# A fused attention and mixture-of-experts kernel: first norms' rows moved to another tile, their transposes to another place in the step, contexts loaded a step sooner, routed products taken from in front of a switch

## The chip, the cores and the metric

The kernel runs on one core of one Trainium2 chip. A core has TensorE (matmuls, called PE in the profile, with its weight loads as PEld), VectorE (DVE), ScalarE (ACT), GpSimd (POOL) and SyncE (SP). SP and POOL also issue DMAs, and each engine works its own instructions in order. The metric is the device time of one execution in microseconds (us); three executions of the kernel before gave 720.6, 720.77 and 722.7, median 720.77.

## The reference

There are 16 batches of 100 tokens with 256 channels, each with a context of 361 rows of 192, and 16 heads of 64.

```python
q = (layernorm(x) @ Wq) heads;  k, v = (ctx @ Wkv) heads
x = x + softmax(q k^T * 64**-0.5) v @ Wproj + bproj
h = layernorm(x)
logits = clip(h @ router_w.T + routing_bias, -50, 50);  probs = sigmoid(logits)
p, sel = top-1 of probs over 7 experts
tw = clip(0.5 + p + 1e-8, 0.5, 2.0)
out = x + 0.5 / tw * swiglu(h, shared) + (p / tw) * swiglu(h, expert sel)
```

`swiglu(h, w1, w2, w3)` is `silu(h @ w1.T) * (h @ w3.T) @ w2.T` with 704 inner channels.

## The kernel before

Everything is fp32. The 1,600 tokens lie in 13 row tiles of 128 (the last has 64), kept in `acc`. `xT` holds the normed tokens transposed, channels on partitions; it feeds the queries, later the router and the shared experts. PSUM is used as eight banks in turn (`bank()`, L125).

**The attention** runs in 32 steps, s = 2b+g: batch b, and g = 0 or 1 for the lower or upper eight heads (L862 to L921). A step has four score products, each for two heads (`scores`, L682). For each, VectorE takes the row maxima (L701), ScalarE the exponentials with their sums (L704), and VectorE then transposes the result in blocks of 32 (L717); that transposing is done one score product later. `moved` (L728) sends the blocks of a whole step through DMAs of SP and POOL into `aT`, which `values` (L750) multiplies with v two steps later for g=0 and one step later for g=1. Between the score products stand products of keys (L611, L632) and values (L611, L659): the keys of batch b+1 and its first value parts in steps with g=1, the rest of the values of b in steps with g=0. So the end of a step with g=0 has three score products in a row. What follows them there, in the order written (PE, ACT, DVE and SP all keep the order in which the code issues):

```python
if g == 0:
    while fillers:            # projections of finished tiles, routers
        fillers.popleft()()
    for _ in range(min(2, len(qs))):
        qs.pop(0)()           # queries, two of four units of two batches
turning(tb)
```

and then `values` of batch b-1, `moved(tb)`, the next context's load (`load_ctx`, L522, at g=1, two batches ahead, into one of two buffers), and `load_later(s)` (L546).

**The norms.** `layer_norm` (L170) returns a list of small parts (moments of each tile, one reciprocal root on POOL, one `normalise` for each tile) and `turn`, the transposes on TensorE (L212) with ScalarE's copies into `xT` (L215). The parts wait in `norms` and are done one after each score product but a step's first, and one at the step's end. When the last part is done, `turn` is put into `turns`; a list of `turns` is worked off at i = 0 of a step with g=0, after the first score product and the product behind it (L899). There are two kinds of norm: the first norm of the input (tiles 0-1, 2-5, 6-8 and 9-12, the last two begun after steps 6 and 9), and the second norm of the attention's result (tiles 0-2, 3-5, 6-8 and 9-12; `keep=True`), whose rows also go to DRAM for the later gather and whose `turn` puts the router (L236) into `fillers`. Both kinds write their rows into `xn`, four buffers in turn (L191). `finished(b)` (L813) puts the projection (L782) of each tile that batch b completes into `fillers`, to be worked off in the next step with g=0.

**The shared experts** follow (`hidden`, `down`, L413 to L508) and overlap with the router of the last group and the sorting of tokens by expert.

**The routed experts** run tile by tile: `run(k)` (L1053) makes the first products of a tile (L1020) into two banks, then the transposes of the next tile's gathered rows (`turn(k+1)`, L976), the rest of the products, and the down product of the tile before (`finish`, L1028). How many tiles there are is data; the kernel reads the number into a register on each engine (L1084) and takes one arm of a `tc.Switch` (L1089), each arm being the whole loop for one number. Before the switch stand, for tile 0, `ahead = turn(0)` between two `down` calls (L1012) and `first_products(0, ahead)` (L1046, L1087): sixteen products.

Of the kernel before, what the change touches and what calls it, by code (L numbers as in the profile page):

```python
# [14 lines left out]
F32 = mybir.dt.float32  # L15
# [7 lines left out]
B, LQ, C = 16, 100, 256  # L23
LKV, CTX = 361, 192
H, DK = 16, 64
I, E = 704, 7
# [38 lines left out]
def xattn_moe(  # L65
# [101 lines left out]

    biases = deque()

    def layer_norm(tiles, keep=False):  # L170


        n = len(tiles)
        of, xns = {}, []

        def moments(i):
            if i == 0:
                of["mv"] = small.tile([P, 4, 2], F32, name="mv")
                of["rstd"] = small.tile([P, 4], F32, name="rstd")
            st = small.tile([P, 6], F32, name="st")  # L180
            nc.vector.bn_stats(st, acc[:, tiles[i], :])
            nc.vector.bn_aggr(of["mv"][:, i, :], st)

        def roots():
            rstd = of["rstd"]
            nc.vector.tensor_scalar(rstd[:, :n], of["mv"][:, :n, 1], EPS, None, ALU.add)
            nc.gpsimd.tensor_tensor(rstd[:, :n], rstd[:, :n], power[:, :n], ALU.pow)

        def normalise(i):
            t = tiles[i]  # L190
            xn = small.tile([P, C], F32, name="xn", bufs=4)  # L191
            nc.vector.tensor_scalar(
                xn,
                acc[:, t, :],
                of["mv"][:, i, 0:1],
                of["rstd"][:, i : i + 1],
                ALU.subtract,
                ALU.mult,
            )
            if keep:  # L200
                nc.sync.dma_start(xn_d[t * P : t * P + rows(t), :], xn[: rows(t), :])
            else:
                biases.append(t)
            xns.append(xn)

        def turn():
            for i in range(0, n, 2):
                tr = bank()
                m = min(2, n - i)
                for o in range(m):  # L210
                    for k in range(2):
                        nc.tensor.transpose(  # L212
                            tr[:, ds((k * m + o) * P, P)], xns[i + o][:, ts(k, P)], ident
                        )
                nc.scalar.copy(  # L215
                    xT[:, :, ds(tiles[i] * P, m * P)],
                    tr[:, : 2 * m * P].rearrange("p (k n) -> p k n", k=2),
                )

        parts = [lambda i=i: moments(i) for i in range(n)] + [roots]  # L220
        return parts + [lambda i=i: normalise(i) for i in range(n)], turn
# [289 lines left out]
    with ExitStack() as attn:  # L511
# [34 lines left out]
        def load_later(s):  # L546

            if 1 < s < 4:
                m = ts(s - 2, NCH // 2)
                nc.sync.dma_start(  # L550
                    wp_sb[:, m], wproj.rearrange("(m p) c -> p m c", p=P)[:, m]
                )
            if s == 3:
                nc.sync.dma_start(rb_sb, rbias.to_broadcast([P, E]))
                nc.sync.dma_start(rw_sb[:, :, :E], rwT.rearrange("(k p) e -> p k e", p=P))
            if s == 4 or s == 7:
                load_x(GROUPS[s // 3 + 1])
            if s == 6 or s == 9:
                normalised(GROUPS[s // 3])
            if 10 <= s < 14:  # L560
                load_shared(s - 10)
            if s in (2 * B - 3, 2 * B - 2):
                load_shared(s - 2 * B + 7)

# [234 lines left out]
        turns, fillers, norms = deque(), deque(), deque()  # L799

        def normalised(g, keep=False):
            parts, turn = layer_norm(g, keep)
            norms.extend(parts)


            def turned():
                turn()
                if keep:
                    fillers.append(lambda: norms.extend(router(g)))

            norms.append(lambda: turns.append(turned))
# [31 lines left out]
        pairs = key_pairs(0)  # L843
        product(pairs)
        product(pairs)
        parts, turn_first = layer_norm(FIRST)
        for one in parts:
            one()
        product(pairs)
# [12 lines left out]
        for s, (b, g) in enumerate(steps):  # L862

            if g == 0:
                pairs = values_of.pop(b)
                if s == 0:
                    ask = lambda: qs.pop(0)() or (lambda: None)
                    pairs[1:] = [ask, ask] + pairs[1:]  # L870
                elif (b + 1) % QG == 0 and b + 1 < B:
                    qs = q_units((b + 1) // QG)
            elif b + 1 < B:
                if b:
                    values_of[b + 1] = value_pairs(b + 1)
                pairs = key_pairs(b + 1)
                for i in (4, 2) if b + 2 < B and b + 1 not in GUESTS else (2,):
                    pairs.insert(i, values_of[b + 1].pop(0))
            else:

                hT0 = ap2.tile([P, NJ, H * DK], F32, name="v")
                hT0 = hT0.rearrange("p j n -> p (j n)")[:, : (NI + 1) * 3 * P]
                hT0 = hT0.rearrange("p (i n) -> p i n", i=NI + 1)
                first = hidden(GROUPS[0], hT0, ap2, 3 * P, SAME)
                pairs = [lambda: first.pop(0)() or (lambda: None) for _ in range(SAME)]
            tb = new_blocks()
            turning = None
            for i in range(n2):
                exponentials, then = scores(b, g * n2 + i)
                if puts:  # L890
                    puts.popleft()()
                exponentials()
                if turning:
                    turning(tb)
                    part()
                turning = then
                for _ in range(-(-len(pairs) // (n2 - i))):
                    product(pairs)
                while g == i == 0 and turns:  # L899
                    turns.popleft()()  # L900
            if puts:
                puts.popleft()()
            if g == 0:
                while fillers:
                    fillers.popleft()()
                for _ in range(min(2, len(qs))):
                    qs.pop(0)()
            turning(tb)
            for _ in range(2 if s < 2 else 1):
                part()  # L910
            if g == 0 and s:
                for at in range(NG):
                    values(b - 1, at, *held.pop(0))
                    after_values()
                finished(b - 1)
            held.append(moved(tb))
            if g == NG - 1 and b + 2 < B:
                cTs[b + 2] = load_ctx(b + 2)
            if g == NG - 1:
                host(b)  # L920
            load_later(s)  # L921
# [62 lines left out]
    with tc.tile_pool(name="hs", bufs=1) as hs:  # L984
        def run_hidden(g):
            n = sum(map(rows, g))
            hT = hs.tile([P, NI + 1, n], F32, name=f"hT{n}")
            for piece in hidden(g, hT, sp):
                piece()
            return hT  # L990

        parts, turn_last = layer_norm(GROUPS[-1], keep=True)
        for one in parts:
            one()
        hT = run_hidden(GROUPS[1])
        turn_last()
        down([(3, hT, 0)])
        for one in router(GROUPS[-1]):
            one()
        down([(5, hT, 2), (4, hT, 1)])  # L1000
        fill = sort_tokens(hs)
        for k in range(NW):
            fetch(k)
        hT2 = run_hidden(GROUPS[2])
        fill()
        for k in range(NX - 1):
            gather_into(xgs, xn_d, k)
        hT3 = run_hidden(GROUPS[3])
        down([(6, hT2, 0), (7, hT2, 1)])
        down([(12, hT3, 3)])  # L1010
        down([(9, hT3, 0), (10, hT3, 1)])
        ahead = turn(0)  # L1012
        down([(8, hT2, 2), (11, hT3, 2)])
    hp = ctx.enter_context(tc.tile_pool(name="hp", bufs=2))

# [27 lines left out]
            oob_is_err=False,  # L1043
        )

    def first_products(k, xgT):  # L1046
        pa, pb = bank(), bank()
        w = wexs[k % NW]
        products(pa, xgT, w, [i * P for i in range(NI - 1)])
        products(pb, xgT, w, [I + HALF + i * P for i in range(NI - 1)])  # L1050
        return pa, pb

    def run(k, state, tiles):  # L1053


        xgT, last, made = state
        w, hT = wexs[k % NW], hTs[k % 2]
        pa, pb = made or first_products(k, xgT)
        pc = bank()
        n = (NI - 1) * P  # L1060
        s = sp.tile([P, n], F32, name="sg")
        nc.scalar.activation(s, pa[:, :n], AF.Silu)
        nc.vector.tensor_tensor(
# [15 lines left out]
            gather_into(bgs, base_d, k + NX - 1)  # L1079
        if k and k + NW - 1 < tiles:  # L1080
            fetch(k + NW - 1)
        return ahead, (k, hT, bgs[k % NX]), None

    n = nc.values_load(e_at[:, NS:], min_val=0, max_val=NS - NF)  # L1084
    for k in range(NX - 1):
        gather_into(bgs, base_d, k)
    first = ahead, None, first_products(0, ahead)  # L1087

    for extra in tc.Switch(n, NS - NF + 1):  # L1089
        then = first  # L1090
# [57 lines left out]
```

## Time and profile before

| | us |
|---|---|
| median of three executions | 720.77 |
| the profiled execution | 721.24 |
| its span, first to last instruction | 719.4 |
| ScalarE, exponentials (L704) | 142.0 |
| VectorE, block transposes (L717) | 132.9 |
| VectorE, maxima (L701) | 123.5 |
| TensorE, keys (L611, 361 columns) | 125.8 |
| TensorE, values' products (L611, 512 columns) | 126.2 |
| TensorE, scores (L688) | 99.2 |
| TensorE, routed products (L1020) | 78.3 |
| TensorE, transposes of normed tiles (L212) | 7.4 |

The last projection of the attention ends at 521 us, the shared experts at 596, and the routed tiles fill the rest. The granted TensorE clock averages 0.995 of full speed. In a list by time, a row gives the start, the duration, the engine, the line, the tiles as out<-in, the shapes and how many instructions were merged; in brackets is the time that the engine was idle before and what ended it. TensorE's matmuls are pipelined, and each fp32 product of the program shows as two, so a row's duration overlaps the next: for what a matmul costs the distance from start to start is read.

### The profile page before, as it was taken

The numbers are of one execution on the slowest core, as the hardware profiler recorded it, in microseconds if no ns is written. First come the engines' busy times: TensorE is split into PE (matmuls) and PEld (weight loads), VectorE is DVE, ScalarE is ACT, GpSimd is POOL, SyncE is SP. The second block draws the span as 40 slices with busy tenths as digits, with TensorE's granted clock in tenths as the row PEclk, the third lists the DMA queues.
The fourth block names the chain that finished last, engine by engine and source line by source line (L and its number), as shares of the span: only waits on it lengthen the run. The fifth ranks groups of instructions, "written<-read, shape, count | busy, mean of one in ns | idle before, by whom it ended". The sixth has DMA issues, their size and how long they took to land. (4 is left out here: it accounts for less than half of the span.)

```text
span 719.4 us, 14826 instructions
## 1 busy us (share of the span) xinstructions
PE 707.9 (98%) x5192; PEld 510.3 (71%) x5192; DVE 420.5 (58%) x1100; ACT 280.7 (39%) x793; POOL 197.3 (27%) x417
## 2 busy tenths in 40 slices
PE   9999999999999999999999999999999998999996
PEld 6556667667575766757577576755866578999996
DVE  2777766867687576876778778677247222122121
ACT  2564563534545263453644636453022111111110
POOL 4142422322342222323223322233010104343321
PEclk9999999999999999999999999999999999999999
DMA  7055756454474543537354473555104912998860
GB/s 260 23 140 157 178 128 159 95 140 125 106 204 127 166 109 96 139 88 197 93 136 124 109 181 83 142 129 143 52 26 155 382 34 58 326 348 333 309 249 23
DMA packets 55979, 109.23 MB, mean 152 GB/s; under 512 B 28681, under 2 KB 37964, under 8 KB 53972
## 3 DMA queue, kind: packets, MB, share of 16 engines
q1 hardware_dynamic: 45252, 81.79, 37.1%
q0 software_dynamic: 10352, 25.98, 13.8%
q8 instruction: 44, 0.72, 0.4%
q14 instruction: 43, 0.35, 0.2%
q10 hardware_dynamic: 288, 0.39, 0.2%
HBM read 60.81 MB, written 5.35 MB: 92 GB/s over the span
## 5 line engine op out<-in xcount | busy, mean ns | idle before, releaser
L704 ACT ACTIVATE at<-mm,nm 128x361 f32<-128x361 f32 x256 | 142.0, 561 | 173.4 <-DVE nm L701 173.2
L738 POOL DMA_DIRECT2D aT<-tb x256 | 126.1, 500 | 296.7 <-PE mm L760 104.6
L701 DVE TENSOR_REDUCE nm<-mm 128x1 f32<-128x361 f32 x256 | 123.5, 523 | 60.1 <-PE mm L688 59.3
L717 DVE STREAM_TRANSPOSE tb<-at 128x384 f32<-128x384 f32 x256 | 132.9, 558 | 4.5
L611 PE MATMUL mm<-cT,wk_sb 64*128 64x361 f32 x768 | 125.8, 467 | 0.5 <-DMA cT<-in_ctxT 0.4
L611 PE MATMUL mm<-wv_sb,cT 64*128 64x512 f32 (+1 forms) x552 | 126.2, 589 | 0.0
L611 PEld LDWEIGHTS mm<-cT,wk_sb 64*128 64x128 f32 x768 | 75.7, 188 | 45.7 <-issue 5.0
L688 PE MATMUL mm<-kT,qT 64*128 64x361 f32 x512 | 99.2, 479 | 1.7 <-ACT at L704 1.7
L611 PEld LDWEIGHTS mm<-wv_sb,cT 64*128 64x128 f32 (+1 forms) x552 | 53.7, 185 | 53.1 <-issue 43.1
L1020 PE MATMUL mm<-xgT,wex 128*128 128x128 f32 x660 | 78.3, 275 | 0.0
L1020 PEld LDWEIGHTS mm<-xgT,wex 128*128 128x128 f32 x660 | 76.9, 192 | 1.0 <-issue 0.3
L688 PEld LDWEIGHTS mm<-kT,qT 64*128 64x128 f32 x512 | 48.8, 188 | 35.8 <-issue 8.9
L760 PE MATMUL mm<-aT,v 128*64 128x100 f32 (+1 forms) x1472 | 72.5, 251 | 0.5 <-DMA aT<-tb 0.4
L760 PEld LDWEIGHTS mm<-aT,v 128*64 128x64 f32 (+1 forms) x1472 | 67.2, 135 | 4.9 <-issue 3.0
L424 PE MATMUL mm<-xT,w_sb 128*128 128x384 f32 (+1 forms) x176 | 60.9, 503 | 0.0
L424 PEld LDWEIGHTS mm<-xT,w_sb 128*128 128x128 f32 x176 | 32.9, 190 | 26.1 <-issue 8.5
L704 ACT ACTIVATION_READ_ACCUMULATOR at<-mm,nm 128x1 f32 x256 | 50.7, 198 | 0.0
L587 PE MATMUL mm<-xT,wq_sb 128*128 128x200 f32 x256 | 46.9, 336 | 0.0
L587 PEld LDWEIGHTS mm<-xT,wq_sb 128*128 128x128 f32 x256 | 43.4, 190 | 4.0 <-issue 1.5
L792 PE MATMUL mm<-wp_sb,resT 128*128 128x256 f32 x192 | 44.8, 386 | 0.0
L651 ACT COPY kT<-mm 128x361 f32<-128x361 f32 x64 | 29.4, 461 | 39.2 <-PE mm L611 39.2
L792 PEld LDWEIGHTS mm<-wp_sb,resT 128*128 128x128 f32 x192 | 35.9, 191 | 10.3 <-issue 2.5
(154 smaller groups left out, 558.9 us busy)
## 6 DMA issues: line engine op xcount, KB each, us to landing
wex<-in_wex SPq DMA_DIRECT2D x15, 2176.0 KB
aT<-tb POOLq DMA_DIRECT2D x256, 80.2 KB, 3.3
aT<-tb SPq DMA_DIRECT2D x256, 80.2 KB
over<-row SPq DMA_DIRECT2D x64, 100.0 KB
cT<-in_ctxT SPq DMA_DIRECT2D x10, 576.0 KB
cT<-in_ctxT SPq DMA_DIRECT2D x5, 541.5 KB
xn_d<-xn SPq DMA_DIRECT2D x12, 128.0 KB
base_d<-acc SPq DMA_DIRECT2D x12, 128.0 KB
```

The source lines that it names most:

```text
L424: nc.tensor.matmul(to[:, :n], w13_sb[:, k, ds(at, P)], xT[:, k, ds(g[0] * P, n)], start=(k == 0), stop=(k == 1),)
L587: nc.tensor.matmul(pq[:, o, :], wq_sb[:, u, k, ts(o, P)], xT[:, k, ts(g, QG * LQ)], start=(k == 0), stop=(k == 1),)
L611: nc.tensor.matmul(to[o][:height, :width], *operands(o, k), start=(k == 0), stop=(k == NR - 1),)
L651: nc.scalar.copy(kT[:, c, :], to[0][:, :LKV])
L688: nc.tensor.matmul(sc[o][:, :LKV], qTs[b // QG][r, c, ts(b % QG, QB), :], kTs[b][c // 4][r, c % 4, :], start=True, stop=True,)
L701: nc.vector.tensor_reduce(nm[:, o : o + 1], sc[o][:, :LKV], AX.X, ALU.max, negate=True)
L704: nc.scalar.activation(at[:, o, :LKV], sc[o][:, :LKV], AF.Exp, bias=nm[:, o : o + 1], accum_out=sums[:, o : o + 1],)
L717: nc.vector.transpose(tb[:, :, :, o, i * QR : i * QR + 32].rearrange("p j k n -> p k j n"), at[:, o, :].rearrange("p (k j n) -> p k j n", ...
L738: queue.dma_start(aT[ts(j, 32), i].rearrange("p k o n -> p (k o n)"), tb[ts(i, 32), j].rearrange("p k o n -> p (k o n)"),)
L760: nc.tensor.matmul(av[ts(o, DK), i, :], v[:n, ds((2 * c + o) * DK, DK)], aT[:n, :, j, o, ts(i, QR)], start=(j == 0), stop=(j == NJ - 1),)
L792: nc.tensor.matmul(pp[:r, :C], resT[:, c, QP : QP + r], wp_sb[:, c, :], start=(c == 0), stop=(c == NCH - 1))
L1020: nc.tensor.matmul(to[:, ts(o, P)], w[:, ds(j * 2 * I + u, P)], xgT[:, j, :], start=(j == 0), stop=(j == 1),)
```

## The change

It has four parts, which keep the arithmetic and the results as they were.

1. `layer_norm` takes a place instead of a flag. The four first norms write their rows into `w13_sb`, the tile that will hold the shared experts' first weights, its two halves in turn (`places`); the second norms keep `xn`. The four loads of these weights (`load_shared`) move from steps 10 to 13 to steps 20 to 23.
2. `turns` are worked off at the end of a step with g=0, before `fillers`, instead of after the step's first score product. Batch 1 keeps the old place. In the order of instructions this moves five groups of transposes behind the step's last score product: tiles 6-8 within step 10; 9-12 from step 14 to step 12; and of the second norms 0-2 from step 16 to 14, 3-5 from 22 to 20, 6-8 from 30 to 28. A router moves with each of the last three, behind the projection and in front of the queries.
3. A context is loaded at the end of the step with g=0 instead of g=1, except the first (b=0).
4. `first_products` is gone. `turn(0)` stands directly before the switch, the sixteen products inside each arm.

```diff
-    def layer_norm(tiles, keep=False):
+    def layer_norm(tiles, place=None):
         n = len(tiles)
+        keep = place is None
...
-            xn = small.tile([P, C], F32, name="xn", bufs=4)
+            xn = small.tile([P, C], F32, name="xn", bufs=4) if keep else place[:, ts(i, C)]
...
-            if 10 <= s < 14:
-                load_shared(s - 10)
+            if 20 <= s < 24:
+                load_shared(s - 20)
...
-            parts, turn = layer_norm(g, keep)
+            parts, turn = layer_norm(g, None if keep else places.pop(0))
...
-        parts, turn_first = layer_norm(FIRST)
+        places = [w13_sb[:, i % 2, :] for i in (1, 0, 1, 0)]
+        parts, turn_first = layer_norm(FIRST, places.pop(0))
...
-                while g == i == 0 and turns:
+                if b == 1 and g == i == 0:
                     turns.popleft()()
             if puts:
                 puts.popleft()()
             if g == 0:
+                while turns:
+                    turns.popleft()()
                 while fillers:
                     fillers.popleft()()
...
-            if g == NG - 1 and b + 2 < B:
+            if g == (NG - 1 if b == 0 else 0) and b + 2 < B:
                 cTs[b + 2] = load_ctx(b + 2)
...
-        ahead = turn(0)
         down([(8, hT2, 2), (11, hT3, 2)])
...
-    def first_products(k, xgT):
-        pa, pb = bank(), bank()
-        w = wexs[k % NW]
-        products(pa, xgT, w, [i * P for i in range(NI - 1)])
-        products(pb, xgT, w, [I + HALF + i * P for i in range(NI - 1)])
-        return pa, pb
-
     def run(k, state, tiles):
-        xgT, last, made = state
+        xgT, last = state
         w, hT = wexs[k % NW], hTs[k % 2]
-        pa, pb = made or first_products(k, xgT)
-        pc = bank()
+        pa, pb, pc = bank(), bank(), bank()
         n = (NI - 1) * P
+        products(pa, xgT, w, [i * P for i in range(NI - 1)])
+        products(pb, xgT, w, [I + HALF + i * P for i in range(NI - 1)])
...
-    first = ahead, None, first_products(0, ahead)
+    first = turn(0), None
```

More of the change, by code (lines that the diff above doesn't have):

```diff
@@ L990, in run_hidden @@
             return hT
-        parts, turn_last = layer_norm(GROUPS[-1], keep=True)
+        parts, turn_last = layer_norm(GROUPS[-1])
         for one in parts:
@@ L1044, in finish, with run @@
         )
-    def first_products(k, xgT):
-        pa, pb = bank(), bank()
-        w = wexs[k % NW]
+    def run(k, state, tiles):
+        xgT, last = state
+        w, hT = wexs[k % NW], hTs[k % 2]
+        pa, pb, pc = bank(), bank(), bank()
+        n = (NI - 1) * P
         products(pa, xgT, w, [i * P for i in range(NI - 1)])
         products(pb, xgT, w, [I + HALF + i * P for i in range(NI - 1)])
-        return pa, pb
-    def run(k, state, tiles):
-        xgT, last, made = state
-        w, hT = wexs[k % NW], hTs[k % 2]
-        pa, pb = made or first_products(k, xgT)
-        pc = bank()
-        n = (NI - 1) * P
         s = sp.tile([P, n], F32, name="sg")
@@ L1081, in run @@
             fetch(k + NW - 1)
-        return ahead, (k, hT, bgs[k % NX]), None
+        return ahead, (k, hT, bgs[k % NX])
     n = nc.values_load(e_at[:, NS:], min_val=0, max_val=NS - NF)
```

## The prediction

> **What bounds the kernel.** I read the page first for who is busy, then TensorE's waits, then its order of time around each place that the change touches.
>
> ```profile
> PE 707.9 (98%) x5192; PEld 510.3 (71%) x5192; DVE 420.5 (58%) x1100; ACT 280.7 (39%) x793; POOL 197.3 (27%) x417
> ```
>
> ```profile
> PE mm L979 <- DVE hgT L1063: 2.0, 1, 2.0
> PE mm L688 <- ACT at L704: 1.7, 1, 1.7
> ...
> PE mm L611 <- DMA cT<-in_ctxT: 0.4, 2, 0.2
> ```
>
> TensorE works 98% of the span, and the waits that the second view names for it (in all, times, longest) come to some 5 us. So two things count alone: TensorE's own work, and any new wait of TensorE. The chain of waits follows only the last output DMA (712 to 716 us) and tells nothing of the rest. A step is s = 2b+g. Most steps have slack, but the end of a step with g=0 has not: three scores stand there in a row, and their exponentials lag. Step 20 in order of time (start, us, engine, line; in brackets the idle time before and what ended it):
>
> ```profile
> 323.43 1.99 PE L688 MATMUL mm<-kT,qT 64*128 64x361 f32 x12
> 325.35 3.72 PE L792 MATMUL mm<-wp_sb,resT 128*128 128x256 f32 x16
> 328.91 2.87 PE L587 MATMUL mm<-xT,wq_sb 128*128 128x200 f32 x16
> ```
>
> ```profile
> 329.51 0.56 ACT L704 ACTIVATE at<-mm,nm 128x361 f32<-128x361 f32 x1 [1.13 <-DVE nm L701]
> ...
> 330.06 0.55 ACT L704 ACTIVATE at<-mm,nm 128x361 f32<-128x361 f32 x1
> 330.51 0.20 ACT L704 ACTIVATION_READ_ACCUMULATOR at<-mm,nm 128x1 f32 x1
> ```
>
> The scores end at T = 325.35, where the projection starts, but ScalarE ends the last exponential at 330.71, T+5.4. VectorE sets that pace: each of the three needs two maxima (L701) and the two transposes of the one before (L717), about 2 us. I call this distance the lag; steps without norm parts (6, 16, 24) have 4.7.
>
> **A. The stall at step 14 goes: -3.3 us.**
>
> ```profile
> 224.05 1.09 PE L212 MATMUL mm<-ident,xn 128*128 128x128 f32 x8
> 225.07 0.88 PE L688 MATMUL mm<-kT,qT 64*128 64x361 f32 x4
> 227.69 3.06 PE L688 MATMUL mm<-kT,qT 64*128 64x361 f32 x8 [1.75 <-ACT at L704]
> ```
>
> ```profile
> 224.60 0.41 DVE L192 TENSOR_SCALAR xn<-acc,mv,rstd 128x256 f32<-128x256 f32 x1 [3.27 <-PE mm L212]
> ```
>
> ```profile
> 228.00:231.40 3.40, 3.40 (x10) 1.87 (x9) 3.24 (x10) 3.25 (x11) 2.71 (x6) 0.50 0.80 206
> ```
>
> VectorE waits 3.27 us at L192: the four xn buffers still hold tiles 9 to 12, untransposed, when the second norm of tiles 0 to 2 wants one. The maxima behind it come late and TensorE idles 1.75 us (1.9 against its usual spacing); then it runs 228.0 to 231.4 at clock 0.50 (the last-but-two number). Start to start against the usual, that window costs 1.4 more. With the first norms' rows in w13_sb nobody holds those buffers. The moved load_shared lands at steps 20 to 23, eight steps before its use at 31.
>
> **B. Contexts a step sooner: -0.9 us.** At 87.2 and 209.0 the first keys start 0.38 us late and the next ones 0.08. The load goes to the end of g=0, behind that step's aT transfers on SP and in front of host and load_later's own; its buffer's last reader, the values of b, is done by then. It leaves the place behind the aT that the next step needs. The values' aT waits at steps 4 and 12 (0.1 and 0.26) may shrink, and one may appear at step 22, whose cover by transposes and router goes: nothing in sum.
>
> **C. Transposes beside projection and queries: -1.4 us.** Before, the products from values to scores take 257.42 to 260.90 with six transposes between them and 320.85 to 323.43 without: 0.90, and the scores behind them take 2.03 instead of 1.92. So 1.01 for six transposes whose own spacing is 0.11 each, 0.66; the rest, 0.35, is paid where TensorE goes from 64-row tiles to 128-row tiles and back. Beside a projection they pay only 0.66. Four groups save 0.35 each. The fifth leaves step 30, where nothing is saved: the second half of its values starts at 479.46 when the aT of step 29 lands, so TensorE waits there instead. At step 28 its 0.66 and its router's 0.47 (266.58 to 267.04) are paid in full: **+1.1 us**. With each router some eighteen small VectorE operations of 0.13 to 0.29 us and one exponential (0.22) come a batch sooner; they are as many as before and go between steps' products as before, except that those at step 29 can put its aT back by up to 0.4 us, within the wait of step 30. The moved transposes pass nothing on SP or POOL.
>
> **E. The new wait: +8.1 us.** In the listed order of the changed program ScalarE's copies of the transposes (L215) stand behind all four exponentials of the step, and the readers follow on TensorE almost at once: the router's L245 at steps 14, 20 and 28, the queries at step 10, because tokens 600 to 799 reach into tile 6. TensorE gets there at T + 0.71 (transposes) + 3.46 (16 spacings of 0.216) = T+4.17. The copies take 0.59 (two tiles), the second ends 0.84 after the lag, and 0.05 is the way to TensorE.
> - Step 10: lag 5.7 (5.77 before, two moments in the way): 5.7+0.59+0.05 = 6.34, wait 2.2.
> - Step 14: only one normalise left in the loop, lag 5.0: 5.89, wait 1.7.
> - Steps 20 and 28: lag 5.36: 6.25, wait 2.1 each.
>
> Step 12 transposes too, but its queries read tokens 600 to 799, long there: none. Behind the waiting matmul stand the queries and the values, and VectorE's last transpose of the step behind their evacuation; the aT made of it is read two steps later, so only TensorE pays. Nothing hides these waits. Banks: eight in turn; the last of step 20's needs the second exponential, which is done at T+3.0.
>
> **D. The switch: -1.1 us**, unknown in part.
>
> ```profile
> 595.70 3.84 PE L1020 MATMUL mm<-xgT,wex 128*128 128x128 f32 x32
> 601.52 0.41 PE L979 MATMUL mm<-ident,xg 128*128 128x128 f32 x2 [1.99 <-DVE hgT L1063]
> ```
>
> ```profile
> L1144 PEldq COMPARE_BRANCH  x1: 3584/3584/3584, 597.7 to 597.7; - x1
> ```
>
> The idle 1.99 us is the branch: TensorE's sequencer is in it from 597.66 to 601.25, and VectorE had finished at 600.6. It reaches the branch 17 matmuls ahead of the array. The change removes no matmul: 16 products stand behind the branch instead of before it. Is that worse? In front of it now stand 15 matmuls of the shared path, so the branch runs under those. The register load (591.97 before, 0.27 earlier now, as two transposes have left; 0.74 long) ends at 592.44; branch from 592.9 to 596.5, first product at 596.8. ScalarE has the transposed rows copied at 596.3, so that is not last. 3.68 us of products: 600.5 against 601.52. Other end: if the branch begins only when the array has drained (595.8), the products start at 599.9 and it is 2.1 slower. A branch at 709.7 took 0.31 us with matmuls still queued, so I take the early end. The Trainium skill ("TensorE: Matmul & The Clock Gate", Architectural detail) gives TensorE a queue of 64; with that the branch would be hidden wholly and the copy decides, -1.5. The trace's 17 matmuls with their 17 weight loads decide. ScalarE's branch moves behind its copy, to 599.8; its silu is late but not needed before TensorE's second tile.
>
> **F. What the waits do to the clock: +4.5 us.** The same page (HAM oscillation) gives a rule that speaks for the change: no idle gaps above about 3.4 us. By it the waits of E cost themselves alone, and the sum is A+B+C+D+E, +1.1 = **+2.5 us**. The trace says otherwise: 1.75 us idle in a window of 3.41 brought half clock for the next; 1.51 us in another (600.0 to 603.4) did not. So the limit is near half a window. There are five gaps of 1.7 to 2.2 us (steps 10, 14, 20, 28, and about 2 at step 30), and each costs 1.5 if 1.6 us of it fall in one window. For a gap of 2.1 that is (3.41-2.1+2x0.5)/3.41, two in three; for 1.7, half. Three windows of five: 4.5 us; none gives 0, all five 7.5.
>
> **Sum.** Against the profiled run's 721.24 (span 719.4 and 1.8 around it): -3.3-0.9-1.4-1.1+1.1+8.1+4.5 = +7.0, 728.2. The median of the runs shown is 0.5 below that run: **727.7 us**, slower by 1.0%.
>
> **Rivals.**
> - *The clock holds* (none or one half window): 723.3 to 724.8. For it: the page's rule, and window phases differ from run to run. Against: the row of A. 0.20.
> - *The copies aren't late*, and the change is faster: the price is E and F, so 721.24-3.3-0.9-1.4-1.1+1.1-0.5 = 715.1. It decides where the lag is below 3.5 us. All sixteen g=0 steps but the first and step 30 show 3.4 to 5.8, and 3.39 is the stalled step 14; the waits together must stay below 5.6 for no loss. 0.08.
> - *The branch starts after the drain*: 3.2 more, 730.9. 0.12.
> - The forecast, two to four half windows, 726 to 729.5: 0.60.
>
> A measurement tells about 0.3% from no change. Faster by more: 0.08; within (718.6 to 722.9): 0.12, the clock holding with a somewhat smaller wait; slower: 0.80. The range 722 to 732 leaves out the second rival and the worst of the third with five windows.
>
> **To check.** Right: no 3.27 us wait at L192 and no half clock near 228; no wait of L611 for contexts; new waits of L245 three times and L587 once on the xT copy, near 2 us; transposes of three tiles followed by L792; two to four rows at clock 0.50 in the attention; first routed product about 1 us behind the last shared one. Wrong: copies that end before the projection does, or a routed product 4 us late.

## The result, and the profile after

| | before | after | ratio, 95% interval |
|---|---|---|---|
| median, us | 721.38 (719.42 to 722.75) | 731.89 (730.7 to 734.83) | 1.015 [1.0124, 1.0176] |
| profiled execution, us | 721.24 | 730.7 | |
| its span, us | 719.4 | 729.0 | |

Each side has six executions; the three that stand ahead of the prediction are among those of the kernel before. The change makes the kernel 1.5% slower. The forecast was 1.0% slower, 727.7 us. The median lies at the upper edge of the range of 722 to 732, and three of the six executions lie above it (732.75, 732.75 and 734.83 us). In the attention every line number of the changed kernel is one higher than before (L212 is now L213).

The first part of the page, engines' busy time, and then TensorE's waits (engine, line, what it waited for: us in total, times, longest), of the kernel after:

```profile
PE 709.2 (97%) x5192; PEld 509.2 (70%) x5192; DVE 421.7 (58%) x1100; ACT 280.8 (39%) x793; POOL 197.4 (27%) x417
```

```profile
PE mm L213 <- DVE xn L193: 6.5, 5, 2.0
PE mm L761 <- DMA over<-row: 2.0, 1, 2.0
PE mm L588 <- ACT xT L216: 2.0, 1, 2.0
PE mm L132 <- DVE ones L129: 1.1, 1, 1.1
PE mm L213 <- DVE w_sb L193: 0.7, 1, 0.7
PE mm L1024 <- DVE acc L506: 0.7, 1, 0.7
PE mm L246 <- ACT xT L216: 0.6, 1, 0.6
PE mm L1024 <- issue: 0.4, 1, 0.4
```

The number of instructions on each engine is unchanged; the time went into waits. The old ones are gone: no L689 waits for L705 (the stall at step 14), no L612 for a context. The largest new one is not where the forecast put it. The router (L246) waits 0.6 us for ScalarE's copies in the whole kernel, where 5.9 were forecast. It is the transposes themselves (L213) that wait, 7.2 us in six pieces, for rows that VectorE has not written yet (w_sb is the new place of the first norms' rows).

Step 20 in order of time, of the kernel after: TensorE, then VectorE, then ScalarE (start, us, engine, line; idle time before in brackets):

```profile
323.08 0.44 PE L213 MATMUL mm<-ident,xn 128*128 128x128 f32 x2
324.43 0.44 PE L213 MATMUL mm<-ident,xn 128*128 128x128 f32 x2 [0.91 <-DVE xn L193]
326.85 0.41 PE L213 MATMUL mm<-ident,xn 128*128 128x128 f32 x2 [1.98 <-DVE xn L193]
327.09 3.62 PE L793 MATMUL mm<-wp_sb,resT 128*128 128x256 f32 x16
330.64 0.54 PE L246 MATMUL mm<-xT,rw_sb 128*32 128x96 f32 x16
```

```profile
324.01 0.37 DVE L193 TENSOR_SCALAR xn<-acc,mv,rstd 128x256 f32<-128x256 f32 x1
324.30 0.96 DVE L702 TENSOR_REDUCE nm<-mm 128x1 f32<-128x361 f32 x2
325.18 0.15 DVE L715 RECIPROCAL at<-sums 128x2 f32<-128x2 f32 x1
325.37 1.04 DVE L718 STREAM_TRANSPOSE tb<-at 128x384 f32<-128x384 f32 x2
326.33 0.37 DVE L193 TENSOR_SCALAR xn<-acc,mv,rstd 128x256 f32<-128x256 f32 x1
```

```profile
328.23 0.20 ACT L705 ACTIVATION_READ_ACCUMULATOR at<-mm,nm 128x1 f32 x1
328.33 0.86 ACT L216 COPY xT<-mm 128x512 f32<-128x512 f32 x2
```

TensorE has finished its scores at T = 323.08. The first row tile was written a step before and is transposed at once. The second and third are written by VectorE at 324.01 and 326.33, each behind the maxima and block transposes of one of the three last score products. So TensorE, which has run ahead of VectorE here, follows it tile by tile. The copies end at 329.19, T+6.1, as forecast (T+6.2). But TensorE has lost its time already: it reaches the router only at T+7.56, and waits for nothing there.

At step 14, where two of the three tiles were written earlier, TensorE meets both waits, a short one for a row and then one for the copies:

```profile
227.56 0.66 PE L213 MATMUL mm<-ident,xn 128*128 128x128 f32 x4
228.94 0.44 PE L213 MATMUL mm<-ident,xn 128*128 128x128 f32 x2 [0.73 <-DVE xn L193]
229.22 3.62 PE L793 MATMUL mm<-wp_sb,resT 128*128 128x256 f32 x16
233.43 0.54 PE L246 MATMUL mm<-xT,rw_sb 128*32 128x96 f32 x16 [0.59 <-ACT xT L216]
```

Here T is 227.56, and the router starts at T+5.87, where the forecast had put it (5.89).

Stretches of 3.41 us, the kernel after (TensorE's busy time, its granted clock, DMA share, GB/s):

```profile
core 0: us, PE busy (x), PEclk, DMA share, GB/s
321.96:325.38 3.42, 2.00 (x12) 1.00 0.84 239
...
444.84:448.25 3.41, 1.48 (x10) 1.00 0.83 245
448.25:451.66 3.41, 2.44 (x7) 0.50 0.59 152
451.66:455.08 3.42, 3.42 (x9) 0.50 0.11 33
455.08:458.49 3.41, 3.41 (x32) 1.00 0.00 0
485.80:489.21 3.41, 1.37 (x32) 1.00 0.71 181
489.21:492.62 3.41, 3.41 (x35) 0.50 0.47 117
```

Step 28 has the same waits as step 20, and at their end TensorE runs two windows at half clock; the wait at step 30 brings a third. This is one execution, the fastest of the six. The three slower ones have mean granted clocks of 0.990, 0.990 and 0.987, against 0.992 here, so they probably had more such windows; they have no trace to show it.

**Where the 9.6 us of the two spans are.** The distances from a step's first score to the next one's, subtracted between the two traces, give a ledger. What the moved instructions cost is taken from the prediction (six transposes 0.66 beside a projection and 1.01 between scores, eight 0.88 and 1.23, a router 0.47); the remainder is wait or clock. The "half clock in the attention" includes 0.5 us that fall into step 31.

| us | forecast | traces |
|---|---|---|
| stall at step 14 and its half window | -3.3 | -3.9 |
| contexts | -0.9 | -1.0 |
| transposes and routers moved | -0.3 | 0.0 |
| wait at step 10 | 2.2 | 2.2 |
| wait at step 12 | 0 | 0.6 |
| wait at step 14 | 1.7 | 1.7 |
| waits at steps 20 and 28 | 2.1 each | 3.4 each |
| half clock in the attention | 4.5 | 4.5 |
| shared experts, switch and routed tiles | -1.1 | -0.7 |
| first score earlier | - | -0.6 |
| sum | 7.0 | 9.6 |

For step 20 the working is: its tail, from the last score to the next step's first, is 4.55 us longer; transposes and router that came into it cost 1.13; 3.42 are wait. At step 28 it is 7.48 longer: 1.13, the same 3.42, and 2.93 for two half windows. At step 14 the wait is read from the router's start (T+5.87 instead of T+4.17). The first score's start is chance: in the profiles of the kernels below it lies between 0.6 us earlier and 0.4 later than before.

### The profile page after: what moved, and what is told of

The parts are those of the page before. It is cut to its first block, busy times and chain, and to the rows that moved or that the text cites. A ratio compares the mean times of both kernels' runs of the same rounds, so it can differ in the third digit from the quotient of the medians.

```text
span 729.0 us, 14796 instructions
## 1 busy us (share of the span) xinstructions
PE 709.2 (97%) x5192; PEld 509.2 (70%) x5192; DVE 421.7 (58%) x1100; ACT 280.8 (39%) x793; POOL 197.4 (27%) x417
## 5 line engine op out<-in xcount | busy, mean ns | idle before, releaser
L705 ACT ACTIVATE at<-mm,nm 128x361 f32<-128x361 f32 x256 | 141.9, 560 | 172.5 <-DVE nm L702 172.3
L612 PE MATMUL mm<-wv_sb,cT 64*128 64x512 f32 (+1 forms) x552 | 126.1, 589 | 0.0
L612 PE MATMUL mm<-cT,wk_sb 64*128 64x361 f32 x768 | 124.8, 464 | 0.1
L612 PEld LDWEIGHTS mm<-cT,wk_sb 64*128 64x128 f32 x768 | 74.1, 187 | 45.7 <-issue 3.0
L689 PE MATMUL mm<-kT,qT 64*128 64x361 f32 x512 | 97.0, 474 | 0.0
L612 PEld LDWEIGHTS mm<-wv_sb,cT 64*128 64x128 f32 (+1 forms) x552 | 52.9, 185 | 53.9 <-issue 43.6
L689 PEld LDWEIGHTS mm<-kT,qT 64*128 64x128 f32 x512 | 48.1, 187 | 35.8 <-issue 9.8
L705 ACT ACTIVATION_READ_ACCUMULATOR at<-mm,nm 128x1 f32 x256 | 50.4, 197 | 0.0
L588 PE MATMUL mm<-xT,wq_sb 128*128 128x200 f32 x256 | 47.1, 337 | 2.0 <-ACT xT L216 2.0
L588 PEld LDWEIGHTS mm<-xT,wq_sb 128*128 128x128 f32 x256 | 43.1, 190 | 6.4 <-ACT xT L216 2.4
L793 PE MATMUL mm<-wp_sb,resT 128*128 128x256 f32 x192 | 46.7, 399 | 0.0
L793 PEld LDWEIGHTS mm<-wp_sb,resT 128*128 128x128 f32 x192 | 37.7, 201 | 8.5 <-issue 2.5
```

The source lines that it names most:

```text
L588: nc.tensor.matmul(pq[:, o, :], wq_sb[:, u, k, ts(o, P)], xT[:, k, ts(g, QG * LQ)], start=(k == 0), stop=(k == 1),)
L612: nc.tensor.matmul(to[o][:height, :width], *operands(o, k), start=(k == 0), stop=(k == NR - 1),)
L689: nc.tensor.matmul(sc[o][:, :LKV], qTs[b // QG][r, c, ts(b % QG, QB), :], kTs[b][c // 4][r, c % 4, :], start=True, stop=True,)
L705: nc.scalar.activation(at[:, o, :LKV], sc[o][:, :LKV], AF.Exp, bias=nm[:, o : o + 1], accum_out=sums[:, o : o + 1],)
L793: nc.tensor.matmul(pp[:r, :C], resT[:, c, QP : QP + r], wp_sb[:, c, :], start=(c == 0), stop=(c == NCH - 1))
```

## The experiments

Each kernel was timed beside the kernel before, whose median was 720.69 us beside turns_back, rows_early, turns_late and switch_alone, 719.20 beside router_late, turns_alone, places_alone and turn0_ahead, and 720.30 beside rows_router and ctx_alone. So kernels of different groups are compared by their ratios, and a difference of less than some 2 us is read from the traces. "Theory 1" is the one formed from the trace above: TensorE waits in two layers, first for VectorE's rows at the transposes, then for ScalarE's copies.

### turns_back: the second part of the change undone

```diff
-                if b == 1 and g == i == 0:
+                while g == i == 0 and turns:
                     turns.popleft()()
...
             if g == 0:
-                while turns:
-                    turns.popleft()()
                 while fillers:
```

> The changed kernel with its second part undone: the transposes stand again after the first score product of a step with g=0; places, contexts and switch stay changed. Theory 1 (all of the loss sits in the moved transposes: 11.1 us of waits at steps 10, 12, 14, 20 and 28 and 4.5 us of half clock): what is left are the gains, 3.6 at step 14, 1.0 at the contexts, 0.7 to 1.1 at the switch, so 715 to 716.5 us, 0.7% faster than before. Rival (part of the loss comes from the places, the contexts or the switch, for instance by the DMAs that they move): 719 us or more.

Measured: 714.81 us, ratio 0.9922 [0.9904, 0.9940]. Its waits:

```profile
PE mm L132 <- DVE ones L129: 1.1, 1, 1.1
PE mm L1022 <- DVE acc L506: 0.8, 1, 0.8
PE mm L761 <- DMA aT<-tb: 0.5, 1, 0.5
```

No window in the attention is at half clock, and steps 15 to 31 start some 5.2 us earlier than before (0.3 of it from the start, 0.9 from the two context waits, 3.9 at step 14). The time lies 0.2 us below what Theory 1 gave and far from its rival. The other three parts together are a gain of 0.8%, and this is the fastest kernel of the study, 2.3% below the changed one by the medians.

### turns_alone: the second part alone on the kernel before

The same edit the other way round: `while turns` at the end of the step, nothing else changed.

> The kernel before with the second part alone (transposes at the end of the step, four xn buffers for all norms as before). Theory 1: the same waits as in the changed kernel, 11 us and 3 to 4 half windows, and the stall at step 14 goes all the same, because tiles 9 to 12 are transposed at step 12: 2 us above the changed kernel, for contexts and switch: 733 us. Rival (without the places, the rows of a later norm wait for a buffer again): a wait at L192 and 736 us or more.

Measured: 731.84 us, ratio 1.0170 [1.0144, 1.0195].

```profile
PE mm L212 <- DVE xn L192: 7.2, 6, 2.0
...
PE mm L760 <- DMA over<-row: 2.1, 1, 2.1
PE mm L587 <- ACT xT L215: 2.0, 1, 2.0
...
PE mm L245 <- ACT xT L215: 0.6, 1, 0.6
```

These are the changed kernel's waits, to within a tenth. At step 14 the time from the first score's start to the last one's end is 4.84 us shorter than before, exactly as in the changed kernel: with tiles 9 to 12 transposed at step 12 the xn buffers are free anyway, and nobody waits at L192 for one. So the first part removes a stall that the second part, too, would have removed. The median lies 1.2 us below the 733 expected; the moved transposes are the whole loss.

### router_late: routers behind the queries, the transposes left where they are

```diff
-                while fillers:
+                for _ in range(len(fillers) - 1 if s in (14, 20, 28) else len(fillers)):
                     fillers.popleft()()
                 for _ in range(min(2, len(qs))):
                     qs.pop(0)()
+                while fillers:
+                    fillers.popleft()()
             turning(tb)
```

> The changed kernel with the routers of steps 14, 20 and 28 behind the queries instead of in front of them; the transposes stay where the change put them. Forecast's theory (TensorE waits at the router for ScalarE's copies, 1.7 + 2.1 + 2.1 us): these 5.9 us go, and step 28 has no half clock: 722 to 726 us. Theory 1 (at steps 20 and 28 TensorE waits earlier, at the transposes, for rows of VectorE, 3.0 us each; the copies are then done before the projection is): only 0.7 us at step 14 go, 0.9 and 2.0 us stay at L213 twice: 731 us.

Measured: 731.48 us, ratio 1.0157 [1.0129, 1.0185], against 1.0150 of the changed kernel: no gain.

```profile
PE mm L213 <- DVE xn L193: 6.5, 5, 2.0
PE mm L761 <- DMA over<-row: 2.1, 1, 2.1
PE mm L588 <- ACT xT L216: 2.0, 1, 2.0
```

The router's 0.6 us at step 14 is gone from the list, and the tail of that step is 0.45 shorter; L213 is untouched. In front of the values 0.3 us of idle time appear at each of the three steps. The profile has three half windows again, though other ones (two behind step 20, one behind step 28, none at step 30). On this run the forecast's account of steps 20 and 28 falls: giving the copies 2.9 us more is worth nothing there while the rows come late.

### rows_early: the rows written a step sooner, TensorE's order untouched

```diff
             load_later(s)
+            for _ in range({11: 2, 13: 2, 19: 3, 27: 3}.get(s, 0)):
+                part()
```

> The changed kernel, with the normalise parts that it leaves to the steps 12, 14, 20 and 28 done at the end of the step before. TensorE's order is untouched; the transposes stand where the change put them. Theory 1 (at steps 12, 20 and 28 TensorE waits at the transposes for rows that VectorE writes between the maxima of the last scores): these waits go, 0.9 to 2.1 us each time at L213, what stays is the wait for ScalarE's copies, 1.4 to 2.2 us at the router or the queries; 2.0 us less at steps 20 and 28, 0.6 at step 12: 727 us, and 724 if the two half-clock windows of step 28 go too. Rival (as forecast: only ScalarE's copies behind the exponentials make TensorE wait, rows cost nothing): 0.6 us less at steps 20 and 28 from the shorter lag, 730.6 us.

Measured: 722.56 us, ratio 1.0021 [1.0010, 1.0031]; 9.3 us below the changed kernel. Waits, and step 20:

```profile
PE mm L246 <- ACT xT L216: 3.6, 3, 1.2
PE mm L761 <- DMA over<-row: 2.1, 1, 2.1
PE mm L588 <- ACT xT L216: 2.0, 1, 2.0
```

```profile
323.48 0.87 PE L213 MATMUL mm<-ident,xn 128*128 128x128 f32 x6
324.19 3.62 PE L793 MATMUL mm<-wp_sb,resT 128*128 128x256 f32 x16
329.00 0.54 PE L246 MATMUL mm<-xT,rw_sb 128*32 128x96 f32 x16 [1.19 <-ACT xT L216]
```

All waits at L213 are gone, and now the router waits for the copies at steps 14, 20 and 28: the forecast's second layer, uncovered. Here its arithmetic holds: the lag is 4.71 (two normalise parts fewer between the maxima), so 4.71+0.84+0.05-4.17 = 1.43; the router starts 1.35 late (1.19 are listed as wait). Against the trace of the changed kernel step 20 is 2.05 us shorter, step 12 0.95, step 14 0.33, and step 28 4.94 (2.0 and the two half windows). The median lies below both numbers expected without and with the half windows (727 and 724). The profile accounts for 7.2 us of span, and step 10's unchanged gap happened to bring a half window in it.

### rows_router: both edits

> Both edits at once: the rows of rows_early and the routers behind the queries. If the wait has two layers (first VectorE's rows, behind them ScalarE's copies), moving the router pays only now: the 1.2 us at the router, three times, go, and with the 2.0 us at step 10's queries and about 2 us at step 30 left, 719 us, 3.6 below rows_early. Rival (the router's wait is no loss of its own, TensorE pays it somewhere behind): 722 us or more.

Measured: 719.78 us, ratio 0.9986 [0.9973, 1.0000].

```profile
PE mm L761 <- DMA over<-row: 2.2, 1, 2.2
PE mm L588 <- ACT xT L216: 2.0, 1, 2.0
```

The edit that gained nothing measurable on the changed kernel takes 1.05 to 1.10 us off each of the steps 14, 20 and 28 here, and 2.8 off the median, near the 719 us expected: two layers, of which the second pays only when the first is gone. What is left are the copies before step 10's queries, the aT at step 30, and 0.34 us in front of the values at each of the three steps.

### turns_late: transposes behind the queries, routers behind the values

```diff
-                if b == 1 and g == i == 0:
+                if (b == 1 or s == 10) and g == i == 0:
                     turns.popleft()()
...
             if g == 0:
-                while turns:
-                    turns.popleft()()
                 while fillers:
...
                     qs.pop(0)()
+                while turns:
+                    turns.popleft()()
             turning(tb)
...
                     after_values()
+                while fillers:
+                    fillers.popleft()()
                 finished(b - 1)
```

> The changed kernel with the transposes behind the queries of the step and their router behind its values (step 10 as before the change, because its queries need the rows). Rows and exponentials are then both finished when TensorE comes to the transposes, about 6.3 us after the scores, and the copies have the values' 3 us. Theory 1 and the forecast: no wait at L213, L246 or L588, no half clock there; 716 us, within 0.7 of the kernel with the transposes at the old place. Rival (transposes and router cost more in a new place by themselves, as switches between row sizes): 718 us or more.

Measured: 717.03 us, ratio 0.9952 [0.9934, 0.9971]. None of L213, L246 and L588 waits. But:

```profile
PE mm L761 <- DMA over<-row: 3.8, 2, 2.5
```

The values at steps 22 and 30 wait for the aT of the step before, 1.3 and 2.5 us, and the latter brings a half window. (The view names `over`, the transfer behind aT's in SP's queue; these products read only aT and v.) The forecast had said that such a wait may appear at step 22, whose cover by transposes and router goes. So even where the moved transposes wait for nothing, the place as a whole gains nothing: it is 2.2 us behind turns_back by the medians, between the two numbers expected. The price is the aT's, not the moved instructions' own. At steps 12 to 16, where no aT is late, the traces show the new place 1.1 us faster.

### places_alone and ctx_alone: the first and the third part alone

The diffs are the hunks shown with the change.

> The kernel before with the first part alone: first norms' rows in w13_sb, its loads at steps 20 to 23. Forecast: the stall at step 14 goes and the half-clock window behind it: 717.3 us, 3.3 to 3.6 us faster (ratio 0.995). Rival (the later loads or the place cost something): less than 2 us faster.

Measured: 716.28 us, ratio 0.9947 [0.9928, 0.9966]. At step 14 the time from the first score's start to the last one's end is 3.6 us shorter and the tail 0.35; the loads at steps 20 to 23 show no wait. As forecast.

> The kernel before with the third part alone: contexts loaded at the end of the step with g=0. Forecast: the waits of the first keys for a context go, 0.9 us: 719.9 us and no L611 in the waits. Rival (the waits come and go from run to run, and the earlier load takes DMA time from the aT transfers): within 0.5 us of before, and longer waits at L760.

Measured: 720.64 us, ratio 1.0001 [0.9987, 1.0015]. No context in its waits, but no gain that can be told either. In the kernels that keep the old load, the wait comes and goes: 0.4 us in two places in the profile of before, 0.7 in one in switch_alone, none listed in turns_alone or places_alone. The 0.9 us read from one profile were partly that execution's.

### switch_alone and turn0_ahead: the switch

switch_alone is the kernel before with the fourth part alone.

> The kernel before with the fourth part alone: no routed products in front of the switch, the transposes of tile 0 directly in front of it. Theory 1 (the branch runs under the shared experts' last products, and 1.8 to 2.0 us of idle TensorE after the first routed products go, 0.7 us of waiting for the copy comes): 719.7 to 720.4 us, 0.1 to 0.15% faster. Rival (the branch starts when the array has drained; or the gain at the first tile is given back at the second): 721 to 723.5 us.

Measured: 718.29 us, ratio 0.9976 [0.9964, 0.9987]. By stages its profile gains 0.92 us between the start of step 31 and the second tile's transposes (3.38 against 2.46 us earlier than before). The changed kernel gains 1.25 there, once the 0.5 us of half clock in its step 31 are taken out. It loses 0.7 of this again in front of a later tile, where TensorE idles 0.4 us and the view names no releaser; ctx_alone, whose switch is the old one, idles 0.6 in the same way. Most of the rest of its 3.5 us of span comes from elsewhere: the first score is 0.6 earlier, and the stall at step 14, which is still there, brought no half window (1.5). The median is lower than expected, and how much of its 2.4 us is the switch it can't tell; the stage says 0.9.

turn0_ahead is turns_back with `ahead = turn(0)` back between the last two `down` calls.

> The kernel of turns_back with the transposes of routed tile 0 back between the two last down products, the routed products still inside the arms. If the branch ends last (in the changed kernel from 603.1 to 606.6 us, first routed product 606.9): TensorE still idles 0.5 to 0.7 us there, 714.5 us. If the copy of the transposed rows ends last (606.67): the idle time goes, and 0.8 us with it: 714.0 us.

Measured: 715.38 us, ratio 0.9937 [0.9917, 0.9957], against 714.81 and 0.9922 of turns_back. Neither of the two expectations came; the idle time in front of the first routed product grows from 0.8 to 1.1 us:

```profile
PE mm L1023 <- DVE acc L506: 1.1, 1, 1.1
```

The copy of tile 0's rows is done 5.7 us before that product here, so it isn't what ends last. The branch is. In the changed kernel, its row (durations shortest, median, longest; first and last start) and TensorE's order:

```profile
L1142 PEldq COMPARE_BRANCH  x2: 326/1901/3476, 603.1 to 719.5; - x2
```

```profile
605.19 0.70 PE L500 MATMUL mm<-w_sb,hT 64*128 64x256 f32 x4
605.82 0.44 PE L984 MATMUL mm<-ident,xg 128*128 128x128 f32 x2
606.94 1.24 PE L1024 MATMUL mm<-xgT,wex 128*128 128x128 f32 x9 [0.68 <-DVE acc L506]
```

603.1 and 3.48 make 606.56; the first product starts at 606.94. In five profiles of this form of the switch (the changed kernel, turns_back, turn0_ahead, switch_alone, rows_router) the branch took 3.48, 3.58, 3.37, 3.86 and 3.87 us, and the first product started 0.38 to 0.45 after its end each time; in the other three the start follows 0.38 after the branch's end as well (rows_early, turns_late, router_late: 3.54, 3.30 and 3.30 us). The view of waits names VectorE's acc as the releaser in most of them, but the products don't read it, and acc ends at no fixed distance: 0.13 to 0.57 us before the product in the five, 0.03 after it in turns_late and router_late. With the transposes directly in front of the switch, 3.2 us of queued matmuls run under the branch in turns_back; in turn0_ahead it is 2.7. So the transposes there are cover for the branch. The branch's own length (3.86 and 3.48) makes the switch's gain 0.9 us in switch_alone and 1.25 in the changed kernel.

## Why the prediction was off in size, point by point

- **A, the stall at step 14**: right. -3.3 forecast, -3.9 in the ledger, and places_alone is 2.9 faster by its median. Not foreseen: the second part alone removes it too.
- **B, contexts**: the waits are gone, the gain isn't measurable alone.
- **C, moved transposes**: -0.3 forecast, 0.0 in the ledger; the aT wait said to be possible at step 22 came, 0.3 us.
- **D, the switch**: right, in size too at its own place (-1.1 forecast, -1.25 at the second tile); the -0.7 of the ledger holds the later loss. The branch starts with matmuls still queued, and the first product starts 1.1 us after the transposes in front of the switch do; the rival "after the drain" would show some 4.
- **E, the new wait: this step failed.** It put TensorE at the router at T + 0.71 + 3.46 = T+4.17. The 0.71 is what six transposes take when their rows are there. At steps 20 and 28 they weren't, and the forecast had put TensorE's wait for them at nothing: the third pair starts at T+3.77, so the transposes take until T+4.01, and the router starts at T+7.56, 3.4 us late instead of 2.1. Step 12, costed at none because its queries need no new tile, waits 0.6 for a row all the same. Step 10 held (2.2), because its rows are finished. Step 14 held in its sum (1.7), since the one late row is hidden behind the later copies. Together 11.4 instead of 8.1 us: these 3.3 are more than the whole gap of 2.6 between forecast and trace; the other terms (last stage +0.4, C +0.3, A and B -0.7, start -0.6) take about 0.6 back. router_late and rows_early show it from both sides.
- **F, the clock**: three windows at 1.5 us, as forecast, but in part by luck: they come from two gaps and not three, and the number is that of one execution. Nor is its limit of 1.6 us sharp: at step 10, 1.73 us in one window brought no half clock.

The evidence was in the forecast's own working. It took the lag of steps 20 and 28 as 5.36, where steps without norm parts have 4.7: two normalise parts stand between the maxima, 0.65 us. It used these two instructions as a delay of the exponentials, and didn't ask who reads what they write: the transposes, which the change brings from the next step but one into the same step. `turns` fills when the last part has been issued, not when VectorE has done it. Before, the distance of two steps covered that; the change takes the cover away.

Of the list to check, the lines on A, B, the order, the rows at half clock and the switch held. Of the four waits near 2 us only L588's came as it was said. And the forecast's own sign of being wrong came at step 20: the copies end at 329.19, the projection at 330.71.

## What to carry to other kernels

When work is moved forward in the written order, find the writer of each of its operands and the place of that writer in its own engine's queue, before costing the work's own readers; a producer that was done "long ago" at the old place may be issued in the same step at the new one. Where an engine has run ahead, as TensorE has at the end of three scores in a row, the places to fill are those whose inputs are a step old. And an edit on one layer of a wait measures nothing while another layer stands in front: the router's move took 0.45 us off step 14 and no wait at L213 off steps 20 and 28 with late rows, and 1.1 us off each of the three steps with early ones.

## What the runs showed of the hardware that was not expected

- **The half clock follows a window that is about half idle.** Counting TensorE's idle time in each 3.41 us window of the twelve profiles, from 30 us to TensorE's last matmul, all twelve windows at full clock with 1.75 us or more idle (1.75 to 2.89) are followed by one at half clock; of five between 1.61 and 1.73 two are; none with 1.47 or less is. The Trainium skill ("TensorE: Matmul & The Clock Gate", HAM oscillation) speaks of idle gaps above about 3.4 us; the measurement decides. So the same gap costs 1.5 us more or not by where the windows fall: step 10's gap, 1.96 to 2.0 us long in every kernel that has it, brought a half window in rows_early and none in the changed kernel. Steps 20 and 28 of the changed kernel have the same two gaps; at step 20 they fell into two windows with 1.42 and 1.47 us, at step 28 1.93 us fell into one.
- **A half-clock window that still held 0.78 us or more of idle time was followed by another.** After 444.84 to 448.25 the next window holds 0.96 us of the gap, and the one behind it, without any, is at half clock too (rows above). The same in router_late (0.78 idle) and turns_alone (1.24). A half window with 0.36 us idle, in turns_alone behind step 20, was followed by full speed, and so were those with none.
- **The branch of a switch takes TensorE's sequencer 3.3 to 3.9 us** in the twelve profiles (on the other engines of the changed kernel 0.04 to 0.07), and starts with 14 to 17 matmuls still queued in front of it. They are its cover. With the transposes in front of the switch the idle time behind them was 0.5 to 1.1 us, as the branch was short or long; without them 1.14.
